# A two-layer vision tower on one core: layer-0 attention's tokens turned by VectorE blocks and DRAM transfers instead of by TensorE

## The chip, the core and the metric

The kernel runs on one core of one Trainium2 chip. Its time is the device time of one launch in microseconds (us). A core has a matrix engine (TensorE, PE in the profile; PEld is its weight load), a vector engine (VectorE, DVE), an activation engine (ScalarE, ACT), a general engine (GpSimd, POOL) and SyncE (SP), which here issues nearly all plain transfers. Sixteen DMA engines move data between DRAM and the on-chip memory SBUF, which has 128 partitions; TensorE writes into PSUM, which has eight banks of 128 x 512 fp32 values. All data are fp32.

## The reference

A batch of 32 images becomes 256 tokens of 256 features each, and these pass two layers. Cut to what matters here:

```python
h = tokens(x)                                   # 16x16 patches times W, plus b
# layer 0, attention, on xn = layernorm(h), then scaled to unit root mean square
uv   = silu(xn @ W_uv + b_uv)                   # 256 -> 512 (u) + 512 (v) + 128 (base)
q, k = base * gamma[0] + beta[0], base * gamma[1] + beta[1]
attn = square(relu(q @ k.T / sqrt(128)))
h    = h + (u * (attn @ v)) @ W_o + b_o
# layer 0, FFN on the top 127 tokens of each image by a router weight
h    = h + scatter(w_sel * ffn(layernorm(h)[top])) + layernorm(h)
# layer 1: phase-memory attention, then a causal 4-head expert attention as FFN
h    = h + attn_1(layernorm(h))
h    = h + ffn_1(layernorm(h))
```

The matmul with `W_uv` contracts over the 256 features. TensorE contracts over partitions, so the normalised tokens, which lie with a token in each partition, have to be turned: features into partitions.

## The kernel before

The 32 images stay in SBUF from end to end, one tile `H[b]` of 128 partitions x (2 token blocks x 256 features) per image. Stage A makes tokens from patches, stage B is the attention of layer 0, stage C its FFN, stages D and E are layer 1. In stages A to D the order of the instructions on each engine is the order in which the program writes them (a manual schedule that covers PE, DVE, ACT, POOL and SP); waits between engines are put in where data or buffers demand them.

Stage B works on pairs of images, 16 pairs in all, and is software pipelined: turn t of its loop (t from 0 to 17) works on pair t (`new`), pair t-1 (`old`), pair t-2 (`older`), and pair t+1 (`next_one`). On PE a full turn is, in this order:

- `turn_b(new)`: eight 128 x 128 transposes of the pair's normalised tokens `cx` into two banks (`transposed`, line 189), which ACT (line 194) and DVE (line 196) copy into `bxT`, 128 features x 2 halves x 512 tokens;
- `turn_weights`: four transposes of router weights (line 483) for two images that are already past the attention;
- `scores_b(old)`, four matmuls from `bq` and `bk`;
- `base_b(new)`, two matmuls of `bxT` with the last 128 columns of `W_uv`;
- `gates_b(old)` and `values_b(old)`, eight matmuls each, which read the `bxT` of the pair before;
- `gated_b(older)` and `output_b(older)`, sixteen matmuls each, half as wide.

Meanwhile DVE compares router weights to rank tokens (lines 390 and 392), makes `bq` and `bk` (lines 270 and 271), normalises the next pair (`norm_b`, line 175, into `cx`), normalises two images for the FFN (line 175 again, and line 376), adds the bias to each value bank (line 439), multiplies the gated products (line 456) and adds the output (line 469). POOL squares the scores (line 421), scatters ranked tokens to DRAM (line 401, indirect transfers), adds `b_o` and the residual to `H` (lines 256 and 383), and computes powers (lines 149 and 150). SP has little to do in the loop: at t=5 and t=7 it loads four ranked images each (`first_ranks`, line 223, tile `cs`).

Turn 0 holds nothing: pairs 0 and 1 are normalised in stage A, where pair 0 is turned too. Turn 1 has no `older`, so it is only scores, base, gates and values; pair 1 is turned at its start. `bxT` has two buffers. `cx` has eight, shared with the FFN's normalised tokens. The pool that holds `cx` (`px`) and the pool of DRAM tiles (`pdram`) live until stage D ends.

## Time and profile before

| | |
|---|---|
| time, median of 3 runs | 1921.87 us (1919.85 to 1925.09) |
| the profiled execution | 1921.73 us, span of the core 1919.9 us |
| busy share of the span | PE 98%, PEld 70%, DVE 65%, ACT 42%, POOL 39% |
| TensorE transposes at line 189 | 256: 144 of `cx`, 112 of `dx` (stage D) |
| of these, into `bxT` in stage B | 15 pairs of 8 |
| copies into `bxT` | 15 on ACT, 585 ns; 15 on DVE, 658 ns |
| one full turn of stage B | 32.30 us |
| stage B | from about 177 to 691 us of the span |
| DMA | 69506 packets, 94.49 MB, mean 49 GB/s |

The profile is one execution of the program. "Busy" adds up the recorded durations of an engine's instructions; PE's are pipelined, so that the records of one run of matmuls overlap, and what one instruction adds to the time is read from the distance between starts. The chain of waits follows the work that ended last back from the end: each step names what released it. Instructions that issue transfers are shown on the queue SPq, and transfers by the packets that the DMA engines moved.

### The profile page before, as it was taken

What the parts mean: (1) busy time and instruction counts of PE and PEld (TensorE: products, weight loads), DVE (VectorE), ACT (ScalarE), POOL (GpSimd) and SP (SyncE); (2) the same over time, 40 slices, a digit from 0 to 9 for tenths busy, and PEclk for the clock granted to TensorE, in tenths of its full rate; (3) what the DMA queues carried; (4) which work ended last, traced back from release to release, by engine and by line L of the source; (5) the groups of instructions that cost most, each with busy time, mean ns of one, the idle gap of its engine ahead of it and who ended that gap; (6) DMA issues with size and microseconds to landing.
All of it is one profiled execution on the core that took longest, in us unless ns stands there. A gap on an engine that the chain in (4) does not pass through costs nothing.

```text
span 1919.9 us, 36937 instructions
## 1 busy us (share of the span) xinstructions
PE 1876.7 (98%) x14852; PEld 1337.1 (70%) x14852; DVE 1255.8 (65%) x3257; ACT 814.9 (42%) x1646; POOL 757.3 (39%) x792
## 2 busy tenths in 40 slices
PE   9999999999999999999999999999999999999993
PEld 8887666666666676766655555568878878787872
DVE  2334456565657573434366556544999999999988
ACT  0001322222222212122343444447787888878772
POOL 1224223333343344334253333334454545455453
PEclk9999999999999999999999999999999999999995
DMA  9450000000000132222000000001222222222212
GB/s 306 152 150 15 1 17 25 25 17 17 15 19 14 41 113 83 61 75 63 12 22 1 1 1 1 1 13 24 60 54 63 57 57 63 52 62 57 63 40 57
DMA packets 69506, 94.49 MB, mean 49 GB/s; under 512 B 8656, under 2 KB 51152, under 8 KB 68944
## 3 DMA queue, kind: packets, MB, share of 16 engines
q1 hardware_dynamic: 62608, 74.49, 13.6%
q0 software_dynamic: 6144, 16.79, 2.8%
q8 instruction: 119, 1.95, 0.4%
q10 hardware_dynamic: 576, 0.79, 0.1%
q14 instruction: 59, 0.48, 0.1%
HBM read 46.41 MB, written 20.97 MB: 35 GB/s over the span
## 4 chain that ended last, share of the span: by engine, by line
PE 95%; DVE 4%; issue 0%; DMA 0%; ACT 0%; POOL 0%; SPq 0%; DVEq 0%; ACTq 0%
PE bank L116 91%; PE bank L772 2%; PE bank L189 1%; DMA patch<-in_patches_dram 0%; PE bank L230 0%; PE bank L483 0%; DVE six L124 0%; DVE fout L1367 0%; DVE fout L1381 0%; DVE eo L1245 0%; DVE ranges L1268 0%; DVE six L967 0%; DVE fout L1370 0%; DVE h L849 0%; DVE ey L1330 0%
## 5 line engine op out<-in xcount | busy, mean ns | idle before, releaser
L1164 POOL TENSOR_SCALAR_AFFINE_SELECT et<-et 128x512 f32<-128x512 f32 (+1 forms) x192 | 165.7, 875 | 203.3 <-ACT et L1155 201.3
L1155 ACT ACTIVATE et<-bank 128x512 f32<-128x512 f32 x384 | 207.7, 630 | 30.6 <-PE bank L116 30.3
L116 PE MATMUL bank<-ev,et 128*64 128x68 f32 (+1 forms) x6144 | 200.6, 226 | 0.0
L116 PEld LDWEIGHTS bank<-ev,et 128*64 128x64 f32 x6144 | 193.1, 138 | 5.7 <-issue 4.7
L116 PE MATMUL bank<-g,sx 64*128 64x512 f32 (+1 forms) x512 | 177.6, 486 | 0.0
L116 PE MATMUL bank<-g,sw 64*128 64x512 f32 (+1 forms) x512 | 177.2, 486 | 0.0
L116 PE MATMUL bank<-tokW,patch 128*128 128x256 f32 x768 | 168.0, 382 | 1.7 <-DMA patch<-in_patches_dram 1.7
L116 PEld LDWEIGHTS bank<-tokW,patch 128*128 128x128 f32 x768 | 146.8, 191 | 23.2 <-issue 2.7
L116 PE MATMUL bank<-bxT,w_wuv 128*128 128x512 f32 x300 | 131.4, 592 | 0.0
L1184 ACT COPY eo<-bank 128x280 f32<-128x280 f32 x256 | 96.1, 395 | 70.1 <-PE bank L116 62.8
L116 PEld LDWEIGHTS bank<-g,sx 64*128 64x128 f32 x512 | 93.1, 187 | 31.8 <-issue 22.9
L116 PE MATMUL bank<-wvo,dm 128*128 128x512 f32 x256 | 114.3, 599 | 0.0
L116 PE MATMUL bank<-attn,bv 128*128 128x256 f32 x512 | 113.1, 379 | 0.0
L116 PE MATMUL bank<-w_wo,gT 128*128 128x256 f32 x512 | 113.1, 379 | 0.0
L116 PE MATMUL bank<-w_w,hT 128*128 128x256 f32 x512 | 113.1, 379 | 0.0
L116 PE MATMUL bank<-xsel,w_w 128*128 128x512 f32 x256 | 111.4, 592 | 0.0
L116 PEld LDWEIGHTS bank<-attn,bv 128*128 128x128 f32 x512 | 97.2, 190 | 19.6 <-issue 6.9
L124 DVE BATCH_NORM_STATS2 six<-h 128x6 f32<-128x256 f32 x256 | 105.5, 412 | 4.4
L116 PEld LDWEIGHTS bank<-w_w,hT 128*128 128x128 f32 x512 | 96.6, 190 | 15.3 <-issue 2.9
L116 PEld LDWEIGHTS bank<-g,sw 64*128 64x128 f32 x512 | 93.1, 187 | 20.1 <-issue 9.9
L116 PEld LDWEIGHTS bank<-w_wo,gT 128*128 128x128 f32 x512 | 97.2, 190 | 13.2
L116 PE MATMUL bank<-w_wuv,bxT 128*128 128x512 f32 x240 | 105.4, 592 | 0.0
(275 smaller groups left out, 3688.8 us busy)
## 6 DMA issues: line engine op xcount, KB each, us to landing
patch<-in_patches_dram SPq DMA_DIRECT2D x31, 768.0 KB, 4.8
sw<-sx SPq DMA_DIRECT2D x64, 128.0 KB, 2.4
out_dram<-fout SPq DMA_DIRECT2D x32, 256.0 KB, 2.7
both<-fxT SPq DMA_DIRECT2D x62, 128.0 KB, 2.3
both<-hx SPq DMA_DIRECT2D x62, 128.0 KB, 2.3
cs<-ranked SPq DMA_DIRECT2D x32, 128.0 KB, 3.0
results<-cy SPq DMA_DIRECT2D x32, 128.0 KB, 1.7
w_w<-in_w_dram SPq DMA_DIRECT2D x2, 1024.0 KB, 8.3
```

Source lines behind the costliest of these rows:

```text
L116: nc.tensor.matmul(o, lhsT, rhs, start=first, stop=last)
L124: nc.vector.bn_stats(six, x)
L189: nc.tensor.transpose(p[:, o : o + P], x[:, c, k * P : (k + 1) * P], ident)
L772: nc.tensor.transpose(p[:, o : o + P], x[:, c, k * P : (k + 1) * P], ident)
L1155: nc.scalar.activation(t2[:, i, :], p, AF.Exp)
L1164: nc.gpsimd.affine_select(out=own, in_=own, pattern=[[0, 2 * n_e], [1, P]], compare_op=ALU.is_ge, fill=0.0, base=0, channel_multiplier=-1,)
L1184: nc.scalar.copy(im.o[:, g * OC : (g + 1) * OC], p[:, 0:OC])
```

## The change

Pairs 2 to 15 are no longer turned by TensorE. As soon as a pair is normalised, in the turn before it is needed, DVE transposes its tokens in blocks of 32 x 32 (two instructions, one for each image), which puts 32 features of a block into 32 partitions with 32 tokens along the row. What remains is to bring the sixteen 32 x 32 blocks of each 128 x 128 into their places across the four groups of 32 partitions. Four transfers on SP write the block rows to a DRAM tile, `b_turned`, with 128 bytes in each contiguous run; four more, later in the same turn, read it into the four partition groups of `bxT` in runs of 2 KB. The reads come in the program after the values of `old`, the last readers of the buffer that they fill. Pair 1 is turned as before (at t=1), and so is pair 0 in stage A. A new SBUF tile `b_blocks` (4 KB per partition) lies in `px`, and two buffers of `b_turned` in `pdram`.

```diff
+    def blocks_b(b0, s):
+        s.d = pdram.tile([32, 16 * NC, 4, 32], F32, name="b_turned", bufs=2)
+        y = px.tile([P, 8, 2 * NC, 32], F32, name="b_blocks", bufs=1)
+        for j, x in enumerate(s.xs):
+            nc.vector.transpose(
+                y[:, :, j * NC : (j + 1) * NC, :].rearrange("p f c t -> p c f t"),
+                x.rearrange("p c (f t) -> p c f t", t=32),
+            )
+        for i in range(4):
+            nc.sync.dma_start(s.d[:, :, i, :], y[32 * i : 32 * i + 32].rearrange("p f c t -> p (f c) t"))
+
+    def turned_b(b0, s, pool, name):
+        s.xT = pool.tile([P, 2, 2 * N], F32, name=name)
+        d = s.d.rearrange("q (k f c) i p -> f q k (c i p)", k=2, f=4)
+        for f in range(4):
+            nc.sync.dma_start(s.xT[32 * f : 32 * f + 32], d[f])
...
         for t in range(B // 2 + 2):
...
-            if new:
+            if t == 1:
                 turn_b(*new, p2, "bxT")
...
             if next_one:
                 norm_b(*next_one)
+                blocks_b(*next_one)
...
             if old and t >= 3:
                 residuals_c(2 * (t - 3))
+            if next_one:
+                turned_b(*next_one, p2, "bxT")
             if older:
                 gated_b(*older)
```

## The prediction

> **What bounds the kernel now.** I read the page's busy shares first, then the chain of waits through one turn of the layer-0 attention loop, then the table of stretches for that turn, then the timelines of two turns, and last the DMA view and the trace's packet records.

> ```profile
> PE 1876.7 (98%) x14852; PEld 1337.1 (70%) x14852; DVE 1255.8 (65%) x3257; ACT 814.9 (42%) x1646; POOL 757.3 (39%) x792
> ```

> ```profile
> 388.50 0.87 PE bank L189 x8
> 389.38 0.44 PE bank L483 x4
> 389.81 30.99 PE bank L116 x108
> 420.81 0.87 PE bank L189 x8
> ```

> The first is a line of the page, the second fence the chain (start us, us, what). TensorE alone carries the chain: a turn is 0.87 us of token transposes (line 189), 0.44 us of weight transposes and 30.99 us of matmuls, and 388.50 + 32.31 is the next start exactly: no gap. A single transpose is recorded with 273 ns, but eight in a row take 0.87 us, so each costs 109 ns of a dense queue.

> ```profile
> core 0: us, PE busy (x) PEld busy (x) DVE busy (x) ACT busy (x) POOL busy (x), PEclk, DMA share, GB/s
> 325.20:357.50 32.30, 32.30 (x122) 21.78 (x121) 20.02 (x58) 7.73 (x12) 12.56 (x12) 1.00 0.08 25
> 357.50:389.80 32.30, 32.30 (x122) 21.78 (x121) 20.03 (x58) 7.74 (x12) 12.47 (x12) 1.00 0.08 25
> ```

> In one turn DVE works 20 of 32.3 us, ACT 8, POOL 12.5, the DMA engines 8% of the time. All but PE have room.

> ```profile
> 364.84 1.38 DVE L175 TENSOR_SCALAR cx<-h,st_b,rs_b 128x256 f32<-128x256 f32 x4
> ...
> 366.13 0.73 DVE L175 TENSOR_SCALAR cx<-h,st_c,rs_c 128x256 f32<-128x256 f32 x2
> ...
> 367.89 4.71 SPq L223 DMA_DIRECT2D cs<-ranked  x2
> ...
> 374.53 7.07 PE L116 MATMUL bank<-attn,bv 128*128 128x256 f32 x32
> ```

> ```profile
> 184.95 2.33 DVE L175 TENSOR_SCALAR cx<-h,st_b,rs_b 128x256 f32<-128x256 f32 x4
> ...
> 188.53 7.03 PE L116 MATMUL bank<-w_wuv,xsel 128*128 128x512 f32 x16
> ...
> 195.40 1.04 PE L189 MATMUL bank<-ident,cx 128*128 128x128 f32 x8
> ...
> 196.27 1.89 PE L116 MATMUL bank<-bq,bk 128*128 128x256 f32 x8
> ```

> Timelines of turn t=7 (weight transposes at 356.91) and of t=1. The next pair is normalised early in a full turn (done at 366.2), but in t=1, which has no gated product and no output projection, only at 187.3, with 8.1 us of matmuls until t=2 begins at 195.4. That short turn decides my number. SP's own queue also shows a block: at t=7 (t=5 alike) the `cs` loads wait for the scatter until 372.6.

> [...]

> **The change, part by part.**

> *PE, removed.* Pairs 2 to 15, 14 pairs of 8 transposes: 112 x 0.109 = 12.2 us, all on the path. The turn should fall from 32.30 to 31.43 us.

> *PSUM copies, removed.* Per pair one ACT copy (585 ns) and one DVE copy (658 ns), off the path: PE waits for neither. A turn takes 18 banks instead of 20; the weight-transposes' bank, held by the rank comparisons for some 7 us, is wanted again by the first value matmul 10.8 us after the turn's start.

> *DVE, added.* Two block transposes of 128x512 per pair. Bounds: 0.54 us (the 128x512 TENSOR_SCALAR, line 270) to 1.3 us (twice the PSUM copy, should the strided output halve the rate). I take 0.65[...]. 1.3 us per pair against 0.66 taken away. Queued behind are the layer-0 FFN norms (line 175), then the value adds (line 439), the first of which had 0.17 us of idle time before it; they fall about 1.3 us back, but each drains a bank every 1.72 us with 0.69 of work, so DVE catches up by the third, and PE wants the first of those banks only some 10 us later. No cost. At worst (2.6 us) it catches up a bank later.

> *SP and DMA, added.* Per pair four writes to DRAM, each 1024 runs of 128 B, then four reads of 64 runs of 2 KB. Over 16 engines that is 256 small and 16 large packets each. Let p be the time of a small packet. Bounds: 13 ns (the packet records' median for 128 B, all reads) and 46 ns (the median of 1 KB packets, which also fits the 340 or so packets per us at the height of the patch loads). I take 26 ns, twice the low end[...]. A write then takes 1.2 us to its first packet and 0.8 us to its receipt (my split of the 2.0 us in which the quickest 128 KB load of `cs` lands) plus 256p, together 2 + 256p = 8.7 us. The read: three further issues 0.45 us apart and 2.7 us to landing (`cs`: 3.0 median, 1.9 least), 4.0 us.

> *The new wait.* `base_b` of the pair now waits for the last read; behind it on PE stand the gates, values, everything. Three kinds of turn, counted from the weight transposes:
> - Full turns (11): DVE starts its ranks 0.4 us later, the blocks are done at 11.0, SP issues at 11.1, and `base_b` is due one turn of 31.43 plus 0.44 plus 1.72 later, at 33.6. Needed: 11.1 + 2 + 256p + 4.0. Slack 16.5 - 256p = 9.8 us; at 46 ns still 4.7. The read's own buffer wait (`bxT` has two, last read by the values) ends at 17.6, earlier. No cost; without this cover each late us costs 11.
> - t=5 and t=7: SP is blocked until 15.7 by `cs`. Slack 11.9 - 256p = 5.2 us; none at 46 ns.
> - t=1: blocks done at 188.7, issue at 188.8; `base_b` due at 195.4 + 1.7 = 197.1 without the transposes. Late by 188.8 + 2 + 256p + 4.0 - 197.1 = 256p - 2.3 = **4.4 us**. At 13 ns 1.0, at 46 ns 9.5. Slow blocks add up to 1.3.

> POOL: the small packets share engines with the scatters of `cx` (line 401), each waiting for the one before; some us of delay push the two POOL adds (5 us) back, still ahead of POOL's next work on the path (line 149, one turn later). No cost.

> Sum against the profiled execution's 1921.73 us (span 1919.9): 1921.73 - 12.2 + 4.4 = 1913.9. Its time is 0.14 below the median shown, so I say **1914 us**, 0.4% less.

> **The rivals.** What a measurement here can tell from no change is about 0.3%, so under 1916.1 counts as faster, over 1927.6 as slower.
> - *Wholly hidden:* t=1 is in time too (p under 10 ns or quicker reads): 1921.7 - 12.2 = 1909.5. For it: the DMA engines stand at 8%. Against: 8.1 us is short for two dependent round trips through DRAM. Chance 0.12.
> - *First turn eats it:* p of 34 to 57 ns. At 46 ns: 1921.7 - 12.2 + 9.5 = 1919.0, within 0.3%. A long PE idle can also drop the clock: the trace has 3.4 us at half clock at 997.7, amid idle stretches, 1.7 us more. Chance 0.18.
> - *The write becomes the bound:* small writes to DRAM dearer than a full 1 KB packet. Sum of late times at t=1, 5 and 7: 3 x 256p - 26.1; it exceeds the gain by 0.3% of the whole (18 us) from p = 57 ns, and from 64 ns every full turn is late as well. At 80 ns: 18.2 + 2 x 8.6 + 11 x 4.0 = 79 us, 1989 us, slower. For it: no row shows such writes[...]. Against: the read of the same size takes 13 ns, and 57 is beyond both bounds. Chance 0.16.

> The forecast itself, p of 10 to 34 ns, has 0.54. That the transposes stay is excluded: line 189 runs for `bxT` only at t=1.

> **How the numbers follow.** Faster is the forecast and "wholly hidden", 0.66; same 0.18; slower 0.16. The forecast's own span is 1909.5 to 1916.1. The range goes from 1908 (0.1 us in a turn either way on 14 pairs) up to 1924, which takes in most of "first turn eats it", and leaves out about 0.2.

> **What would show it.** Right: 32 matmuls at line 189 for `cx` (144 now), turns 31.43 us apart in the chain, a DVE transpose row of 28 near 0.65 us, one DMA wait of PE near 197 us, about 4 us, and none later; 128 B packets near 26 ns. Wrong: a PE wait for `bxT` in each turn (the write is the bound), turns of 32.3 us (the transposes were covered), or waits of PE for DVE (the block transposes are not).

## The result, and the profile after

The changed kernel takes 1912.82 us (median of 5 runs, 1910.74 to 1913.65), against 1921.87 us (by now also of five): a ratio of 0.995, 95% interval 0.9935 to 0.9964. The interval lies wholly below 1, so it is faster, by 9.05 us or half a per cent. The profiled execution took 1911.49 us, with a span of 1909.7.

The page's busy shares, and the chain of waits through two full turns of stage B (start us, us, what):

```profile
PE 1864.9 (98%) x14740; PEld 1323.7 (69%) x14740; DVE 1313.2 (69%) x3271; ACT 805.8 (42%) x1632; POOL 757.6 (40%) x792
```

```profile
322.69 0.44 PE bank L500 x4
323.12 30.99 PE bank L116 x108
354.11 0.44 PE bank L500 x4
354.55 30.99 PE bank L116 x108
385.54 0.44 PE bank L500 x4
```

PE has lost 112 matrix instructions, exactly the transposes. A turn is 0.44 + 30.99 = 31.43 us, the 0.87 us of token transposes are gone, and the next turn follows without a gap. (Line numbers after the new functions are larger by 17 to 20: line 483 has become 500, 439 is 456, 456 is 473.) DVE's busy time has risen by 57.4 us, of which the new transposes less the saved copies make only some 10.

The table of stretches for the same two turns:

```profile
core 0: us, PE busy (x) PEld busy (x) DVE busy (x) ACT busy (x) POOL busy (x), PEclk, DMA share, GB/s
322.70:354.10 31.40, 31.40 (x114) 20.88 (x113) 25.52 (x58) 7.05 (x11) 12.54 (x12) 1.00 0.24 59
354.10:385.50 31.40, 31.40 (x115) 20.88 (x113) 25.53 (x58) 7.05 (x11) 12.54 (x12) 1.00 0.24 59
```

PE is full, DVE works 25.5 us of a turn instead of 20.0, and the DMA engines 24% instead of 8%.

Then the timelines. First turn t=7, whose weight transposes start at 353.95:

```profile
363.99 1.29 DVE L266 STREAM_TRANSPOSE b_blocks<-cx 128x512 f32<-128x512 f32 x2
...
365.07 4.28 SPq L223 DMA_DIRECT2D cs<-ranked  x2
...
369.45 2.99 SPq L271 DMA_DIRECT2D b_turned<-b_blocks  x4
...
375.13 2.62 SPq L277 DMA_DIRECT2D bxT<-b_turned  x4
...
387.55 1.02 PE L116 MATMUL bank<-bxT,w_wuv 128*128 128x512 f32 x2
```

The blocks are done 11.3 us into the turn; SP can issue the writes only when the `cs` loads are out, at 15.5; the reads are issued from 375.13, and `base_b` takes their data at 387.55, on time. Then the short turn t=1 and the start of t=2:

```profile
185.14 1.29 DVE L266 STREAM_TRANSPOSE b_blocks<-cx 128x512 f32<-128x512 f32 x2
...
186.45 3.06 SPq L271 DMA_DIRECT2D b_turned<-b_blocks  x4
...
192.59 2.51 SPq L277 DMA_DIRECT2D bxT<-b_turned  x4
193.34 1.89 PE L116 MATMUL bank<-bq,bk 128*128 128x256 f32 x8
...
197.72 10.43 PE L116 MATMUL bank<-bxT,w_wuv 128*128 128x512 f32 x20 [2.50 <-DMA bxT<-b_turned]
```

Here the round trip is late: PE waits 2.50 us. It is the only wait of PE for `bxT` in the trace:

```profile
PE bank L116 <- DMA bxT<-b_turned: 2.5, 1, 2.5
```

But look at the duration beside it. The next 20 matmuls take 10.43 us; in all later turns the same 20 take 8.75. The table of stretches says why (after the wait, and after that):

```profile
197.72:201.20 3.48, 3.48 (x5) 1.56 (x6) 0.00 (x0) 0.00 (x0) 0.00 (x0) 0.53 0.02 5
201.20:206.00 4.80, 4.80 (x13) 2.17 (x12) 3.95 (x8) 2.06 (x3) 1.99 (x2) 1.00 0.00 0
```

The granted clock (the share of TensorE's full clock, which the trace records) was 0.53 in the stretch after the wait: 3.4 us at half clock, which cost another 1.7 us.

To set variants apart I use the length of stage B in each trace, from the start of the last patch matmuls to the first FFN matmuls. Before:

```profile
172.17 5.34 PE L116 MATMUL bank<-tokW,patch 128*128 128x256 f32 x24
...
691.60 7.03 PE L116 MATMUL bank<-xsel,w_w 128*128 128x512 f32 x16
```

And after:

```profile
170.11 5.34 PE L116 MATMUL bank<-tokW,patch 128*128 128x256 f32 x24
...
681.65 7.03 PE L116 MATMUL bank<-xsel,w_w 128*128 128x512 f32 x16
```

This length excludes the spread of the first 170 us: in all executions but e8's, stage B starts between 170.11 and 172.53 us, and this gave the changed kernel's profiled execution 2.06 us before the change had begun. The times of e1 to e8 were measured beside other runs of the kernel before, with medians of 1921.36 us (e1, e2, e3, e5) and 1921.14 us (the rest), and the ratios given with them are to those.

| kernel | stage B, us | against before | time, us |
|---|---|---|---|
| before | 519.43 | | 1921.87 |
| changed | 511.54 | -7.89 | 1912.82 |
| pair 2 on TensorE (e1) | 508.08 | -11.35 | 1910.36 |
| pair 2 prepared early (e5) | 507.20 | -12.23 | 1909.19 |
| added work beside the old path (e2) | 519.44 | +0.01 | 1922.05 |
| two issuing queues (e3) | 510.39 | -9.04 | 1913.90 |
| writes three times (e6) | 520.76 | +1.33 | 1922.62 |
| e1 with writes six times (e4) | 595.49 | +76.06 | 1996.62 |
| e5 with blocks after the norms (e7) | 507.21 | -12.22 | 1909.23 |
| e5 with transposes three times (e8) | 507.61 | -11.82 | 1911.04 |

### The profile page after: what moved, and what is told of

Read it like the earlier page. It is cut to its first block, busy times and chain, and to the rows that moved or that the text cites. A ratio compares the mean times of both kernels' runs of the same rounds, so it can differ in the third digit from the quotient of the medians.

```text
span 1909.7 us, 36912 instructions
## 1 busy us (share of the span) xinstructions
PE 1864.9 (98%) x14740; PEld 1323.7 (69%) x14740; DVE 1313.2 (69%) x3271; ACT 805.8 (42%) x1632; POOL 757.6 (40%) x792
## 4 chain that ended last, share of the span: by engine, by line
PE 94%; DVE 4%; issue 1%; ACT 0%; DMA 0%; SPq 0%; POOL 0%; DVEq 0%; ACTq 0%
PE bank L116 91%; PE bank L792 2%; PE bank L189 1%; PE bank L230 0%; PE bank L500 0%; DVE six L124 0%; DVE fout L1387 0%; DVE fout L1401 0%; DVE eo L1265 0%; DMA b_turned<-b_blocks 0%; DVE ranges L1288 0%; DVE six L987 0%; DVE fout L1390 0%; DMA bxT<-b_turned 0%; DVE h L869 0%
## 5 line engine op out<-in xcount | busy, mean ns | idle before, releaser
L116 PE MATMUL bank<-ev,et 128*64 128x68 f32 (+1 forms) x6144 | 198.9, 225 | 0.0
L116 PEld LDWEIGHTS bank<-ev,et 128*64 128x64 f32 x6144 | 191.5, 137 | 5.7 <-issue 4.7
L116 PE MATMUL bank<-g,sx 64*128 64x512 f32 (+1 forms) x512 | 177.6, 486 | 0.0
L116 PE MATMUL bank<-g,sw 64*128 64x512 f32 (+1 forms) x512 | 177.2, 486 | 0.0
L116 PE MATMUL bank<-tokW,patch 128*128 128x256 f32 x768 | 167.6, 381 | 0.0
L116 PEld LDWEIGHTS bank<-tokW,patch 128*128 128x128 f32 x768 | 146.6, 191 | 21.4 <-DMA tokW<-in_tokW_dram 0.7
L116 PE MATMUL bank<-bxT,w_wuv 128*128 128x512 f32 x300 | 133.0, 598 | 2.5 <-DMA bxT<-b_turned 2.5
L116 PEld LDWEIGHTS bank<-g,sx 64*128 64x128 f32 x512 | 93.1, 187 | 31.6 <-issue 22.7
L116 PE MATMUL bank<-wvo,dm 128*128 128x512 f32 x256 | 114.3, 599 | 0.0
L116 PE MATMUL bank<-attn,bv 128*128 128x256 f32 x512 | 113.1, 379 | 0.0
L116 PE MATMUL bank<-w_wo,gT 128*128 128x256 f32 x512 | 113.1, 379 | 0.0
L116 PE MATMUL bank<-w_w,hT 128*128 128x256 f32 x512 | 113.1, 379 | 0.0
L116 PE MATMUL bank<-xsel,w_w 128*128 128x512 f32 x256 | 111.4, 593 | 0.0
L116 PEld LDWEIGHTS bank<-attn,bv 128*128 128x128 f32 x512 | 97.2, 190 | 19.6 <-issue 7.2
L116 PEld LDWEIGHTS bank<-w_w,hT 128*128 128x128 f32 x512 | 96.6, 190 | 15.3 <-issue 2.9
L116 PEld LDWEIGHTS bank<-g,sw 64*128 64x128 f32 x512 | 93.1, 187 | 20.1 <-issue 9.9
L116 PEld LDWEIGHTS bank<-w_wo,gT 128*128 128x128 f32 x512 | 97.2, 190 | 13.2
L116 PE MATMUL bank<-w_wuv,bxT 128*128 128x512 f32 x240 | 105.4, 592 | 0.0
```

Of the source, the lines that this page charges most:

```text
L116: nc.tensor.matmul(o, lhsT, rhs, start=first, stop=last)
```

## The experiments

**Is the loss all in the first turn?** Pair 2 back on TensorE:

```diff
-            if t == 1:
+            if t in (1, 2):
                 turn_b(*new, p2, "bxT")
...
-                blocks_b(*next_one)
+                if t > 1:
+                    blocks_b(*next_one)
...
-            if next_one:
+            if next_one and t > 1:
                 turned_b(*next_one, p2, "bxT")
```

> Pair 2 is turned on TensorE like pair 1, so the short first turn needs no transfer; pairs 3 to 15 stay with blocks and DRAM. Theory (112 transposes of 0.109 us gained, one late read at t=2 that costs 2.5 us of waiting and about 1.7 us of half clock after it): 104 transposes gained, 11.3 us, no wait for bxT, no half clock near 200 us, so about 1910.5 us, some 3 us under the changed kernel, and t=2 takes 31.9 us from the end of the values of t=1 to the next turn. Rival (the missing 4 us are spread over the turns, by work that DVE or the transfers slow down): the eight transposes come back, 1913.5 us or more. Second rival (the half clock has nothing to do with the wait): it stays, and only 1.6 us are won.

Measured: 1910.36 us, ratio 0.9936 (0.9922 to 0.9949). Stage B is 11.35 us shorter than before; 104 transposes of 0.109 us are 11.3. No wait for `bxT`, clock at full from the start of stage B to its end. The loss was in that one turn, wait and half clock together, and nothing is spread over the others.

**Can the first turn be covered?** Pair 2 normalised, transposed and written in stage A, where its statistics have long been there:

```diff
+            if b == B - 3:
+                norm_b(4, pairs_b[2])
+                blocks_b(4, pairs_b[2])
...
-            if next_one:
+            if next_one and t > 1:
                 norm_b(*next_one)
                 blocks_b(*next_one)
```

> Pair 2 is normalised, block-transposed and written to DRAM in stage A (after image 29), its read at t=1 finds the data there. Theory: the late read at t=2 goes, nothing else changes, the full 12.2 us are gained: about 1909.7 us, some 4 us under the changed kernel, 0.9 under the one with pair 2 on TensorE, no half clock near 200 us. Rival (DVE in the tail of stage A has no room for 2.8 us more, or the writes disturb the last patch loads): stage A ends later by 1 to 3 us, and 1911 to 1913 us come out.

Measured: 1909.19 us, ratio 0.9929 (0.9916 to 0.9943), stage B 12.23 us shorter: 112 x 0.109 = 12.2, the whole of it. The rival's 1911 to 1913 did not come: at the end of stage A, PE waits 0.66 us for DVE, as in the changed kernel. The interval of its ratio and that of the changed kernel overlap a little (the medians are 3.6 us apart), but by stage B it beats both kernels: 507.20 us, where three executions of the changed kernel (two of them further down) took 509.92 to 511.68. Both have lost the same 112 transposes, so this difference is what the late read costs: 4.34 us in the execution shown above.

**Is the added work free?** Transposes, writes and reads for all 14 pairs, with `bxT` still made by TensorE and the reads put into the tile of the blocks, where nobody looks:

```diff
-            if t == 1:
+            if new:
                 turn_b(*new, p2, "bxT")
...
-        s.xT = pool.tile([P, 2, 2 * N], F32, name=name)
+        xT = s.y.rearrange("p f c t -> p (f c t)").rearrange("p (k n) -> p k n", k=2)
...
-            nc.sync.dma_start(s.xT[32 * f : 32 * f + 32], d[f])
+            nc.sync.dma_start(xT[32 * f : 32 * f + 32], d[f])
```

Here `s.y` is the tile of the blocks.

> All fifteen pairs are turned on TensorE as before and those tiles are used; the block transposes, the writes and the reads of pairs 2 to 15 are made beside them, into a tile that nobody uses (the blocks' own). Theory (all of the added work is covered): the time of the kernel before, 1922 us within 0.15%, turns of 32.30 us. Rival (the added DVE work or the packets slow the loop): each turn over 32.30 us, up to 0.7 us more, up to 10 us in all.

Measured: 1922.05 us, ratio 0.9999 (0.999 to 1.0007); stage B 519.44 us against 519.43. All of the added work is covered, and the whole gain is the transposes' own PE time. (The late read at t=2 is no part of this test: nothing waits for it here.)

**What makes the round trip long?** Two of the four writes and reads issued by ACT:

```diff
-            nc.sync.dma_start(s.d[:, :, i, :], y...)
+            (nc.sync, nc.scalar)[i % 2].dma_start(s.d[:, :, i, :], y...)
...
-            nc.sync.dma_start(s.xT[32 * f : 32 * f + 32], d[f])
+            (nc.sync, nc.scalar)[f % 2].dma_start(s.xT[32 * f : 32 * f + 32], d[f])
```

> Of the four writes and the four reads of a pair, two each are issued by ACT instead of SP. Theory (part of the wait at t=2 is issue time: SP takes 0.67 us for a write and 0.6 for a read, one after the other): about 1.2 us less for the reads and up to 1.3 for the writes, the wait at t=2 falls from 2.5 us to some 0 to 1.2 us; if a wait of that size still ends in 3.4 us at half clock, 1910 to 1912 us, if not, 1909.5 to 1911. Rival (the packets set it, 3.8 us for 4096 of them at 13 ns over 16 engines): the wait falls only by the reads' part, to about 1.3 us. ACT, which waits for the writes before it goes on to its silus, should cost nothing: PE needs those only a turn later.

This missed: the wait did not fall, it rose to 2.95 us. Its timeline shows both reasons:

```profile
188.41 1.39 SPq L271 DMA_DIRECT2D b_turned<-b_blocks  x2
...
194.57 1.32 SPq L277 DMA_DIRECT2D bxT<-b_turned  x2
...
196.21 0.63 ACT L457 ACTIVATE bv<-bv 128x512 f32<-128x512 f32 x1 [1.09 <-DVE bv L456]
196.35 1.25 ACTq L277 DMA_DIRECT2D bxT<-b_turned  x2
```

From the first write's issue to the first read's are 6.16 us, with one queue 6.14 (186.45 to 192.59): issue in halves does not bring the writes home sooner. It ended the issue sooner (at 190.08, 1.7 us after the first, instead of 3.1), but the 4096 packets still span 3.85 us, as with one queue (3.77): for the writes the rival was right, the packets set it. And ACT's reads stand behind the last silu of the values in ACT's order and leave at 196.35, later than any of SP's before. I had written that ACT would cost nothing; the cost is that its own queue is late, in just the turn that has no room. (Its time, 1913.90 us, is no better than the changed kernel's, though its profiled execution had no half clock and a shorter stage B.)

**How much slack have the full turns?** Each pair's writes issued three times (to three DRAM tiles, the last one read), on the changed kernel:

```diff
+        for more in range(2):
+            d = pdram.tile([32, 16 * NC, 4, 32], F32, name=f"b_more{more}", bufs=2)
+            for i in range(4):
+                nc.sync.dma_start(d[:, :, i, :], y[32 * i : 32 * i + 32].rearrange("p f c t -> p (f c) t"))
         for i in range(4):
             nc.sync.dma_start(s.d[:, :, i, :], y...)
```

> The changed kernel with every pair's four writes issued three times, to three DRAM tiles, of which the last is the one that is read. Theory (a full turn has over 8 us of slack for the round trip): 8192 packets more take 8 to 9 us more, the full turns still wait for nothing, t=5 and t=7 at most 1 us each; only the read at t=2, which has no slack, is later by those 8 to 9 us: PE waits 10 to 12 us there once, 1921 to 1924 us in all. Rival (the slack in the full turns is about used up): a wait for bxT in each turn, 1950 us and more. On the clock: if a long PE wait is what halves it for 3.4 us, it must be seen after this one.

Measured: 1922.62 us, ratio 1.0003 (0.9994 to 1.0013). PE waits 9.3 us at t=2, a little less than forecast, and 0.49 when it wants the reads of t=7, nowhere else in stage B:

```profile
206.95 11.88 PE L116 MATMUL bank<-bxT,w_wuv 128*128 128x512 f32 x20 [9.30 <-DMA bxT<-b_turned]
```

The packets of a pair now span 11 to 12 us instead of 3.8 to 4.6, and a full turn takes that without a wait. As foreseen, the clock fell, for 10.24 us (three times 3.41).

And six times, on the kernel without the late first read (the same edit with `range(5)`, on e1):

> The kernel with pair 2 on TensorE (no late read at t=2), with every pair's writes issued six times, the last set being the one that is read. Theory (slack of a full turn near 10 us, packets of 13 ns over 16 engines, so 3.3 us or more for each set): five sets more cost 17 to 19 us, 7 to 9 us over the slack; the first full turn waits that long for bxT, later ones on average about half of it, since a late base also makes the next block transposes late: 30 to 60 us over the 1910 us of that kernel. If SP's issue (24 times 0.68 us) sets it and not the packets, the first wait is 2 to 4 us and the whole 10 to 25 us more. Rival (the round trip is nowhere near the limit): no waits, 1910 us.

Measured: 1996.62 us, ratio 1.0396 (1.0375 to 1.0417). The packets of a pair span 22 us; the first late turn waits 5.11 us, between what I gave for the packets and what I gave for SP's issue:

```profile
232.47 11.12 PE L116 MATMUL bank<-bxT,w_wuv 128*128 128x512 f32 x20 [5.11 <-DMA bxT<-b_turned]
```

```profile
PE bank L116 <- DMA bxT<-b_turned: 59.7, 13, 8.0
```

The waits add up to 59.7 us, but the forecast, 30 to 60 us for the whole, missed: stage B grew by 87.4 us over e1. Most of the other 27.7 us is the clock. It was at half for 61 us of stage B, 3.4 or 6.8 us with most of the waits; PE idled for 12 us of them, and half speed over the other 49 costs about 25. The rest fits 0.24 us that every wait cost beyond its recorded length (again_1, below: 2.48 us of waiting, no half clock, and a stage B 2.72 us longer than that of e5). So the write can become the bound, and each us of waiting then costs about 1.5.

**What lengthens DVE?** In the changed kernel single DVE instructions of 0.4 us take 4.4 (turn t=6):

```profile
335.66 4.38 DVE L175 TENSOR_SCALAR cx<-h,st_c,rs_c 128x256 f32<-128x256 f32 x1
...
341.96 2.47 DVE L456 TENSOR_TENSOR bv<-bank,rows_b 128x512 f32<-128x512 f32 x4
344.35 1.87 DVE L473 TENSOR_TENSOR gT<-bank,uT 128x512 f32<-128x512 f32 x3
```

The first bias add of the values comes 19.4 us into the turn (weight transposes at 322.52), where the kernel before had it at 12.7; then DVE runs without a pause to catch up. The same add in the kernel before (weight transposes at 324.61):

```profile
337.27 0.69 DVE L439 TENSOR_TENSOR bv<-bank,rows_b 128x512 f32<-128x512 f32 x1 [0.17 <-PE bank L116]
```

While the long instruction lasts, POOL adds to `h`:

```profile
336.15 2.50 POOL L256 TENSOR_TENSOR h<-h,rows_b 128x512 f32<-128x512 f32 x2
338.60 1.27 POOL L400 TENSOR_TENSOR h<-h,cx 128x512 f32<-128x512 f32 x1
```

The long one starts while POOL issues an indirect transfer (335.18 to 336.14). POOL's first three adds follow that without a gap, and it ends at 340.03, just after the third (339.87). Two edits on e5. The blocks after the norms instead of ahead of them:

```diff
                 norm_b(*next_one)
-                blocks_b(*next_one)
             if old and t >= 3:
                 norms_c(2 * (t - 3))
+            if next_one and t > 1:
+                blocks_b(*next_one)
```

> The kernel with pair 2 prepared early, and the block transposes placed after the two FFN norms in DVE's order. In the changed kernel the norms fall 1.3 us back and then run while POOL adds to h, and single DVE instructions of 0.4 us take 4.4 us. Theory (the collision with POOL's adds makes DVE 6 us late, and PE is just still covered): DVE's busy time falls by some 40 to 47 us, the bias adds of the values start again near 13 us into the turn instead of 19, and the time stays at that of the kernel with pair 2 early, 1909 us within 0.1%. Rival (the lengthened instructions come from the packets of the writes): they stay, wherever the transposes stand.

Measured: 1909.23 us, ratio 0.9944 (0.9927 to 0.996), stage B 507.21 against 507.20. DVE's busy time falls from 1314.8 us (e5) to 1269.0, by 45.8, and the bias adds of the values start 14.5 us into the turn. One turn (t=13) still has such an instruction, of 5.43 us. The packets are the same, so the lengthening does not come from them; and the kernel before, whose stage B has no 128 B packets, has one too, 5.44 us at 595.38. It follows where the norms fall against POOL's adds: the longer the row of adds without a gap, the longer the hold, 1.48 us with one add (at 340.30 in the changed kernel), 2.66 with two (e8), 4.38 with three, 5.44 with four (the kernel before). In these traces the held DVE instruction did not end between adds of 1.27 us that followed each other without a gap, only once the row was over (at 340.03 in the changed kernel, 0.16 us after the third add). What in the chip holds it, no run here shows.

And the transposes three times over at the old place:

```diff
-        for j, x in enumerate(s.xs):
+        for j, x in list(enumerate(s.xs)) * 3:
             nc.vector.transpose(
```

> The kernel with pair 2 prepared early, with each block transpose made three times (2.7 us more of DVE per pair, at the same place). Theory (DVE's lag of 6 us leaves PE 1.4 us: the second gated product is ready 1.4 us before the output matmuls that read it): DVE is later by 1 to 3 us, PE waits 0 to 1.5 us in each of the eleven or so turns that have FFN norms, 1909 to 1925 us, with PE waits for DVE in the list. Rival (DVE catches up with room to spare, as I forecast): no PE wait, 1909 us.

Measured: 1911.04 us, ratio 0.995 (0.993 to 0.997). One PE wait grew in stage A, 2.1 us instead of 0.7 for DVE's copy of `xsel`; the tripled transposes of pair 2 stand ahead of it there. In stage B PE waits for DVE once, 0.14 us at 597.71 (t=14), and the stage takes 507.61 us, 0.41 more than in e5. So neither side came out as written, but the cover is used up. In the ten turns before that (t=4 to t=13) DVE runs without a pause through all four gated products (t=6, weight transposes at 321.46):

```profile
345.04 2.48 DVE L476 TENSOR_TENSOR gT<-bank,uT 128x512 f32<-128x512 f32 x4
```

The first product ends at 345.72, and TensorE loads it as weights for the output matmuls at 345.78, 0.06 us later. In e5 these two are 1.6 to 1.9 us apart. DVE's 2.4 us more work made the bias adds only 1.8 us later (21.2 us into the turn); the held instruction is shorter here. My later fear of a cover of 1.4 us had about the right size; the forecast, that DVE catches up with room to spare, had not.

**When does a wait halve the clock?** The changed kernel itself, profiled again:

> The changed kernel, unaltered, profiled once more, for the clock after the wait at t=2. If a wait of 2.5 us always halves the clock, 3.4 us at half clock follow it here too and stage B takes 511.5 us from the last patch matmuls to the first FFN matmuls. If it depends on where the wait falls[...], some executions have it and others not, and a stage B without it takes 509.8 us.

> The same once more: the wait for bxT at t=2 is 2.5 us again, since its two round trips depend on nothing that changes between executions; the half clock after it may be there or not, as in the run before this one.

Both waited, 2.48 and 2.55 us, and one of them paid for it:

```profile
199.41 8.82 PE L116 MATMUL bank<-bxT,w_wuv 128*128 128x512 f32 x20 [2.48 <-DMA bxT<-b_turned]
```

```profile
198.78 10.52 PE L116 MATMUL bank<-bxT,w_wuv 128*128 128x512 f32 x20 [2.55 <-DMA bxT<-b_turned]
```

Stage B was 509.92 and 511.68 us, as expected for the two cases. In the trace's clock record all half-clock stretches that end within the trace are multiples of 3.413 us, and the changes of the clock lie on one grid of that step (to 0.001 of a step): in the changed kernel they come 1, 235, 237 and 490 steps after the first, in the kernel before 1, 250, 251 and 261. This grid can be laid over the waits, to read how long PE idled within one window, that is, one step of it:

| execution | PE idle in a window, us | clock after it |
|---|---|---|
| again_1 | 0.97, then 1.51 | full |
| e3 | 1.35, then 1.60 | full |
| e6, first window | 1.81 | full |
| changed | 2.34 | half |
| again_2 | 2.55 | half |
| e6, second window | 3.41 | half |

In these, up to 1.81 us idle of a window left the clock alone and 2.34 halved it. The thirteen waits of e4 narrow this: windows with 1.86 and 1.99 us idle left it alone, windows with 2.02 and 2.15 halved it. (Over the whole length of all twelve traces both outcomes occur between 1.83 and 1.99 us; the ends of matmuls are modelled, so the last digits are rough.) Once halved, the clock came back after a window with 0.34 us idle (e4), and not after windows with 0.66 (e6) or 0.68 (e4). So a window idle for some 60% was enough here, and whether a wait of 2.5 us paid 1.7 us more went with where it fell in the grid. Why the clock follows such a grid, no run here shows.

The profile before already held both cases, in stage D:

```profile
986.49 4.54 PE L116 MATMUL bank<-dxT,w_wk 128*128 128x512 f32 x6 [2.43 <-DVE dxT L196]
...
1012.01 2.41 PE L116 MATMUL bank<-dxT,w_wk 128*128 128x512 f32 x5 [2.55 <-DVE dxT L196]
```

The first wait lies in one window, and half clock follows it, from 986.8 to 990.2 us of the span. (This is the stretch that the prediction puts at 997.7, which is a time of the clock record and not of the span.) The second wait is longer, but falls into two windows, 1.27 and 1.29 us, and the clock stays at full.

## Why the prediction was right, and where its sum was not

1914 us was forecast, 1912.82 measured, 8 us of gain against 9.05. Step by step:

- *PE, removed: 12.2 us.* Right. The turn fell from 32.30 to 31.43 us, and e5 gained 12.23.
- *Copies, banks.* Right: no wait of PE for either.
- *DVE, added: 0.65 us a transpose, "catches up by the third", no cost.* The size, my estimate between two bounds, was right (0.685, 28 of them), the cost too (e2: 0.01 us). The working was not: I let DVE fall 1.3 us back, and it fell 6.7, since I moved its norms in time without asking what POOL does then. DVE caught up only in the gated products. The cover was work of PE, and it was enough, by 1.6 to 1.9 us at the first gated product; e8 used it up.
- *p = 26 ns.* Twice too large: the 57344 new packets of 128 B have a median of 13 ns, the low bound. That a write would take twice as long as a read of its size was my estimate, which no trace had shown; the doubling is not there in the time of these writes.
- *The write, 2 + 256p = 8.7 us.* Measured 5.5 us from issue to landing (186.45 to 191.95), as p = 13 ns gives (5.3): 1.3 to the first packet, 3.8 of packets, 0.4 to the last receipt.
- *The read, 4.0 us.* Too small: 0.64 us from the landing to SP's first read, 0.6 us of issue each instead of 0.45, 3.1 to landing, altogether 5.6.
- *The late read at t=1: 4.4 us.* It was 2.5: too much for the write and too little for the read, partly against each other. The half clock after it, 1.7 us, was in a rival as a thing that "can" happen after a long idle; it happened in two of three executions, after 2.5 us. Wait and half clock together, 4.34 us against e5, came close to 4.4 for a reason that the sum did not have: this is luck.
- *Slack of full turns 16.5 - 256p.* At 13 ns 13.2 us; measured at t=6 10.2 (the last read lands at 345.9, `base_b` takes it at 356.1). The sum had the read 1.6 us too short, and in such a turn, with scatters beside them, the packets span 4.6 us, not 256 x 13 ns = 3.3. The last write of t=6 lands at 340.25 and the values end at 340.30, so that the read's two conditions end all but together. e4's 18.3 us of added packets were late by 5.1, in the turn t=2, which has no rank comparisons and so issues earlier. At t=7, the last read lands at 380.2 and is wanted at 387.55: 7.3 us, where I gave 5.2 at 26 ns and p = 13 gives 8.6.

Of the rivals, "wholly hidden" failed by 2.5 us, and e5 shows that it takes only an earlier start. "First turn eats it" had the right place. "The write becomes the bound" is real, but not at one write: it took the sixfold packets, and its price was too low, since no wait carried its half clock.

## What to carry to other kernels

Where TensorE bounds a stage, an operation taken off it was worth its spacing in a dense queue (0.109 us here, not the recorded 0.273: e5 gained 12.23 us from 112), and work put on other engines cost nothing (0.01 us of stage B in e2) as long as each turn had time for it. A busy share does not show how much time that is: DVE was busy 27 of 31.4 us in e8, and its cover was used up. So look for the one turn that is shorter than the rest, and prepare its data a stage earlier. A DMA round trip through DRAM, 4096 small runs out and 256 large ones back, took 11.3 us from first issue to use and belongs behind at least as much work. When an instruction moves in time, ask not only who waits for it but what runs beside it then.
